# Ten kept-row slots, a new pace for the node tiles and evenly handed early products in the max-pooling layer of a graph network

## The chip, the cores and the metric

The kernel runs on one core of a Trainium2 chip. The metric is the device time of one execution in microseconds: the median of 3 runs, 2517.03 us (2515.44 to 2526.33). The core's engines run side by side, each through its own list of instructions in order: PE (matrix products; PEld is its weight load), DVE (vector), ACT (scalar), POOL (which issues the gathers) and SP (which issues plain transfers). They meet at semaphores.

## The reference

`x` has 6250 rows of 256, and 100000 edges lead from `src` to `dst` with `dst` sorted. The block is a layer norm with ReLU, then four graph layers and a last product:

```python
h = jnp.maximum(_layernorm(x, axis=-1), 0.0)
# layer 1, mean:   h @ W1_self + (segment_sum(h[src]) / deg) @ W1_neigh + b1
# layer 2, pool:   hp = relu(h @ W_pool + b_pool); hmax = segment_max(hp[src])
#                  h @ W2_self + hmax @ W2_neigh + b2
# layer 3, gcn:    ((segment_sum(h[src]) + h) / (deg + 1)) @ W3_neigh + b3
# layer 4, mean:   h @ W4_self + (segment_sum(h[src]) / deg) @ W4_neigh + b4
x = x + (h @ W_fc + b_fc)
```

All features inside are 512 wide. Layer 2 alone has a nonlinearity inside (the ReLU and the maximum). From its output on everything is linear, so the kernel multiplies the later weights into each other and carries layer 2's result times those products, in rows of 512 numbers.

## The kernel before

**Tiles and steps.** The 6250 nodes make NT = 49 tiles of 128; the edges make T = 782 groups of 128. Few low nodes take most edges (`dst` grows as a square), so sums into the first tiles ("hub" tiles) are done as products with a count matrix, whose blocks of 128 by 128 lie in `tab_a`; sums into the others gather rows.

**Prologue (to about 93 us).** Loads `x` in 17 groups of three tiles, normalizes them, turns the edge lists around (`pt_e`, `srcT`), finds where windows of edges begin (`pa`, with `SN` as input), and computes two weight products with `W2_pool` (`w2pf`): `pt_w` turns a weight block on PE, ACT copies it (`wT`), `pm_w` multiplies, ACT copies the result (`Wa`, `Wb`). A generator `products1` hands these steps out: line 1186 says how many after each group `g`. Layer 1 follows (to about 648 us).

**Layer 2, the pooling stage (about 648 to 1850 us).** One loop over 782 steps, counted by `at`, in six blocks from the last to the first (100, 130, 180, 220, 100 and 52 steps). Each step gathers 128 rows (POOL, L1803, into `X`, two steps to a buffer, six buffers) and takes running maxima on DVE (L1784); every second step SP stores a row of maxima (L1788). When a block ends, its *carry* goes from partition to partition: PE turns the last maxima (`ptcf`, L1524), DVE scans them, PE turns them back, and a row is stored. After that the node tiles whose edges begin in that block can be finished.

**Node tiles (`done2`, from tile 48 down to 1; tile 0 has its own function).** A tile gathers its maxima (`tot`, L1658), takes the maximum of two of them if its edges cross a block (DVE, L1678), turns them on PE (L1682), and multiplies with the merged weights in eight f32 products (L1689 and L1692 for its own part, L1695 for the maxima). ACT splits the result into a high part (`hi`, L1702) and a low part (`lo`, L1711). `row_parts(d)` says where these go: tiles 40 to 48 into a small pool, the others into slot `d % 11`, of which slots 0 to 7 lie in the tile `kept_rows` and three in a pool `early3`. Tiles 0 to 7 must end in `kept_rows`, since layer 3 reads them there. A tile is begun when it is ready, at least 11 steps have passed (7 in the last block) and fewer tiles are begun than `NT * (at - 112) / (T - 36 - 112)`, a straight line from step 112 to 746.

**Early products.** Layer 3 needs, for each of 23 hub tiles, a product over all node tiles. For node tiles 8 to 39 it is done early, inside the pooling stage: four finished tiles make a batch, and a batch gives 23 groups of four *pairs* (736 pairs in all). For each group SP loads blocks (`ae`, L1752, fourteen buffers), ACT widens them (`aw`, L1739), PE does pairs (L626 in f16 and L631 in f32), and DVE adds the sum to `acc` (L1435; the first batch is copied by ACT instead). For the hub tile's own row the pair is joined by two more products. From step 321 on, each step asks for a 48th of the pairs that are waiting (fewer steps near the end). A slot may be overwritten when all pairs of the tile that held it have been handed out; `over` has that number and an assertion checks it.

**What sets the order.** The code is written in the order above; a scheduler then orders the instructions of each engine by its own estimates. The order of SP, POOL, PE and ACT below is its result; DVE's in the prologue is fixed by hand.

## Time and profile before

| | |
|---|---|
| median of 3 runs | 2517.03 us (2515.44 to 2526.33) |
| profiled execution | 2523.93 us, span 2522.0 us, mean granted clock 0.933 |
| prologue and layer 1 | to about 648 us |
| pooling stage, first gather to last | 653 to 1803 us |
| layers 3 and 4 | about 1850 to 2522 us |
| busy share of the span | PE 86%, DVE 80%, POOL 69%, ACT 50% |

All positions are microseconds from the first instruction of the profiled execution. Busy time counts instructions that execute; an engine that waits for a semaphore is idle, and the bracket behind a row tells how long it had been idle and what ended that. A busy share near 1 tells that an engine has no gaps, not that nothing else could go faster.

### The profile page before, as it was taken

How to read it: one execution, taken by the hardware profiler on the slowest of the kernel's cores; microseconds unless marked ns; L12 is line 12 of the kernel's file. 1: busy time of each engine (PE TensorE's matmuls, PEld its weight loads, DVE VectorE, ACT ScalarE, POOL GpSimd, SP SyncE). 2: the span in 40 equal slices, each digit the busy share in tenths (PEclk: the TensorE clock that was granted, in tenths of full speed). 3: DMA queues.
4: the chain of work that ended last, by engine and by line, in shares of the span. 5: the costliest groups of instructions: out<-in, count | busy, mean ns of one | idle time of the engine just before them, and what ended most of it. 6: DMA issues, size and time to landing. Idle time of an engine off the chain costs nothing.

```text
span 2522.0 us, 35297 instructions
## 1 busy us (share of the span) xinstructions
PE 2158.2 (86%) x9402; PEld 1248.5 (50%) x9402; DVE 2010.3 (80%) x5565; ACT 1273.2 (50%) x2569; POOL 1729.6 (69%) x2013
## 2 busy tenths in 40 slices
PE   4699999999795565769999999896389999799997
PEld 2456666776443232334444444343244444477776
DVE  7899987785799898888889999798757777467665
ACT  4888888676488787765323333231112222244443
POOL 5477776667566777676667665677477777477775
PEclk9799999999897787789999999898799999899999
DMA  9677777777899999999999999999799999899997
GB/s 306 198 231 233 223 210 213 216 235 238 294 364 303 341 350 346 323 367 357 334 307 339 342 335 301 299 361 326 258 395 407 407 407 407 319 359 333 335 310 234
DMA packets 381357, 785.68 MB, mean 312 GB/s; under 512 B 56430, under 2 KB 175830, under 8 KB 381116
## 3 DMA queue, kind: packets, MB, share of 16 engines
q0 software_dynamic: 135184, 471.64, 56.0%
q1 hardware_dynamic: 158504, 221.70, 24.4%
q10 hardware_dynamic: 87460, 90.01, 10.7%
q8 instruction: 76, 1.25, 0.2%
q14 instruction: 133, 1.09, 0.1%
HBM read 573.99 MB, written 209.94 MB: 311 GB/s over the span
## 4 chain that ended last, share of the span: by engine, by line
PE 45%; DMA 27%; DVE 14%; issue 5%; ACT 5%; POOL 4%; ACTq 0%; DVEq 0%; POOLq 0%; SPq 0%
DMA X<-rows,srcIf 9%; PE pd L626 8%; PE pd L631 8%; PE pd L624 6%; DMA xq<-acc 5%; PE pm_prf L1695 3%; DVE run L1784 3%; DMA ring<-tab_s,srcE 3%; PE pm_hp L1271 3%; PE pm_prf L1689 2%; DMA rows<-X 2%; PE pm_hp L1265 2%; POOL X L1803 2%; PE pm_prf L1692 2%; PE pg L568 2%
## 5 line engine op out<-in xcount | busy, mean ns | idle before, releaser
L1803 POOL DMA_INDIRECT X<-rows,srcIf x782 | 742.7, 950 | 346.1 <-issue 148.8
L1784 DVE SCALAR_TENSOR_TENSOR run<-run,samef,X 128x512 f32<-128x512 f32 x758 | 572.9, 756 | 31.8 <-DMA X<-rows,srcIf 27.0
L548 POOL DMA_INDIRECT ring<-tab_h,srcT x402 | 389.6, 969 | 177.6 <-issue 39.9
L1912 ACT CAST af<-ac 128x640 fp32r<-128x640 fp8e4 (+2 forms) x299 | 217.2, 734 | 339.3 <-PE pd L624 121.7
L548 POOL DMA_INDIRECT ring<-tab_r,srcE x254 | 255.0, 1004 | 102.8 <-issue 35.1
L1784 DVE SCALAR_TENSOR_TENSOR X<-X,samef,run 128x512 f32<-128x512 f32 x379 | 281.9, 744 | 40.2 <-issue 19.7
L548 POOL DMA_INDIRECT ring<-tab_s,srcE x254 | 244.5, 963 | 93.0 <-issue 23.5
L602 DVE SCALAR_TENSOR_TENSOR acc<-pg,M,acc 128x256 f32<-128x256 f32 (+2 forms) x556 | 281.3, 533 | 31.6 <-PE pg L573 16.3
L573 PE MATMUL pg<-ring,hot 128*128 128x256 f32 (+1 forms) x656 | 292.2, 455 | 0.0
L631 PE MATMUL pd<-kept_rows,aw 128*128 128x512 f32 x529 | 271.0, 588 | 0.0
L1739 ACT CAST aw<-ae 128x512 fp32r<-128x512 fp8e4 x184 | 113.8, 620 | 252.1 <-PE pd L631 225.0
L570 PE MATMUL pg<-ring,hot 128*128 128x259 f16 (+1 forms) x656 | 211.5, 325 | 28.7 <-DMA ring<-tab_r,srcE 8.3
L626 PE MATMUL pd<-kept_rows,ae 128*128 128x512 f16 x529 | 208.5, 394 | 10.7 <-DMA ae<-tab_a 8.4
L1695 PE MATMUL pm_prf<-unf,hTf 128*128 128x512 f32 x384 | 196.9, 637 | 6.1 <-ACT hTf L1685 5.4
L631 PE MATMUL pd<-Z1h,af 128*128 128x256 f32 x588 | 194.8, 364 | 1.0 <-ACT af L1299 1.0
L544 DVE TENSOR_SCALAR hot<-iota_bf,keyE 128x128 fp32r<-128x128 bf16 x508 | 138.3, 300 | 48.2 <-PE pg L573 22.7
L624 PE MATMUL pd<-zt,af 128*128 128x512 f32 x598 | 166.3, 398 | 1.5 <-ACT af L1912 1.5
L626 PEld LDWEIGHTS <-ae 128*128 128x128 fp8e4 x736 | 71.3, 97 | 193.0 <-issue 176.6
L626 PE MATMUL pd<-Z1l,A 128*128 128x259 f16 x588 | 158.5, 280 | 0.0
L573 PEld LDWEIGHTS pg<-ring,hot 128*128 128x128 f32 x656 | 130.7, 199 | 47.7 <-issue 39.1
L624 PE MATMUL pd<-z,af 128*128 128x512 f32 x529 | 149.1, 400 | 2.8 <-ACT af L1912 1.5
L463 ACT ACTIVATE A<-pb 128x392 fp8e4<-128x392 f32 x240 | 116.2, 495 | 69.7 <-PE pb L457 65.7
(439 smaller groups left out, 5027.7 us busy)
## 6 DMA issues: line engine op xcount, KB each, us to landing
rows<-X SPq DMA_DIRECT2D x385, 256.0 KB
rows<-hpf SPq DMA_DIRECT2D x49, 256.0 KB
th<-tab_t ACTq DMA_DIRECT2D x49, 256.0 KB
X<-rows,srcIf POOLq DMA_INDIRECT x782
ae<-tab_a SPq DMA_DIRECT2D x184, 64.0 KB
tab_a<-A ACTq DMA_DIRECT2D x15, 784.0 KB
ac<-tab_a ACTq DMA_DIRECT2D x138, 80.0 KB
tab_t<-th SPq DMA_DIRECT2D x37, 256.0 KB
```

Source lines behind the costliest of these rows:

```text
L544: nc.vector.tensor_scalar(hot[j], iota_b, keyT[:, j - jb : j - jb + 1], None, op0=ALU.is_equal)
L548: nc.gpsimd.indirect_dma_start(out=ring[:, j % deep, :].bitcast(F32), out_offset=None, in_=table, in_offset=bass.IndirectOffsetOnAxis(ap=s ...
L570: nc.tensor.matmul(pg[:, : F + counts], hot[j].bitcast(BF16)[:, 1::2], X.bitcast(F16)[:, 2 * F : 3 * F + counts], start=(k == 0), stop=False)
L573: mm = nc.tensor.matmul(pg[:, :F], hot[j], X[:, :F], start=False, stop=(k == n - 1))
L602: nc.vector.scalar_tensor_tensor(acc[d], half, m, acc[d], op0=ALU.mult, op1=ALU.add)
L624: nc.tensor.matmul(hold[0], a[0], z, start=(s == ss[0]), stop=(s == ss[-1]))
L626: nc.tensor.matmul(hold[0][:, : F + extra], a[1], z[1][:, : F + extra], start=(s == ss[0]), stop=False)
L631: nc.tensor.matmul(hold[0][:, :F], a[0], z[0], start=False, stop=(s == ss[-1]))
L1695: nc.tensor.matmul(pm, hT[:, c, :], un[:, c, :], start=False, stop=(c == KH - 1))
L1784: nc.vector.scalar_tensor_tensor(put, held, st, row, op0=ALU.mult, op1=ALU.max)
L1803: nc.gpsimd.indirect_dma_start(out=X[:, k, :], out_offset=None, in_=tab_p, in_offset=bass.IndirectOffsetOnAxis(ap=srcI[:, t : t + 1], axis=0),
L1912: nc.scalar.copy(wide[i][:, :n, :], got[i][:, :n, :])
```

## The change

Five edits, all in the fast path:

1. `SLOTS = (10, 13)`: ten slots in `kept_rows` and 13 in all, where there were 8 and 11. A table `slot` is made for every tile: tiles 39 down to 4 take 0, 1, 2 ... 12, 0 and so on; tiles 3 to 0 take 0 to 3. `kept_rows` takes over the place of the merged weights' tile, which is as large, so no other tile is moved by it.
2. Instead of an assertion, `row_parts` hands out early products until the slot's former tile is done.
3. `PACE`: the limit on begun tiles is now a line with two kinks, 0 at step 112, 19 at step 318, 37 at 612, 49 at 746 (the straight line has 15.9 at 318 and 38.6 at 612). The least distance of 11 or 7 steps is kept.
4. From step 321 on, the early products handed out follow a straight line over all 736 pairs from step 320 to step 742, bounded by what is ready, in place of a 48th of what is waiting.
5. In the prologue the steps of `products1` begin at group 4, not 3, and two of them come with each of groups 7 to 13, not 7 to 12.

```diff
-FIRST_AT = 112
 EARLY_AT = 310
+SLOTS = (10, 13)
+PACE = ((112, 0), (318, 19), (612, 37), (746, 49))
...
-                for _ in range(2 if 7 <= g < 13 else g >= 3):
+                for _ in range(2 if 7 <= g < 14 else g >= 4):
                     next(steps, None)
...
         def row_parts(d):
-            i = d % ROWS3
-            assert early.done >= over.get(d + ROWS3, 0)
+            i = slot[d]
+            if d in held_by:
+                early.advance(over[held_by[d]])
...
-            if i < KEPT:
+            if i < SLOTS[0]:
                 return kept_rows[0][:, i, :], kept_rows[1][:, i, :]
...
-        ROWS3 = 2 * BATCH + 3
+        slot, held_by, last = {}, {}, {}
+        for d in reversed(range(NT)):
+            slot[d] = i = (EARLY[1] - 1 - d) % SLOTS[1] if d >= 4 else 3 - d
+            assert d >= KEPT or i < SLOTS[0]
+            if d < EARLY[1]:
+                if i in last:
+                    held_by[d] = last[i]
+                last[i] = d
+        assert all(d >= EARLY[0] for d in held_by.values())
+        early_all = H3 * (EARLY[1] - EARLY[0])
...
+        def paced(at):
+            for (a0, n0), (a1, n1) in zip(PACE, PACE[1:]):
+                if at < a1:
+                    break
+            return n0 + (n1 - n0) * (at - a0) / (a1 - a0)
...
-                        kept_rows += [span3.tile([P, KEPT, FH], dt, tag=f"kept{i}",
+                        kept_rows += [span3.tile([P, SLOTS[0], FH], dt, tag=f"kept{i}",
...
                     if at > EARLY_AT + 10:
-                        early.advance(early.done + math.ceil(
-                            early.left() / max(1, min(48, T - 24 - at))))
+                        early.advance(math.ceil(early_all * (at - EARLY_AT - 10)
+                                                / (T - 40 - EARLY_AT)))
...
-                            and begun2 < NT * (at - FIRST_AT) / (T - 36 - FIRST_AT)):
+                            and begun2 < paced(at)):
...
-            Z3 = {s: (kept_rows[0][:, s, :], kept_rows[1][:, s, :]) for s in range(KEPT)}
+            Z3 = {s: tuple(v[:, slot[s], :] for v in kept_rows) for s in range(KEPT)}
```

What this does to the engines' lists is shown at three places. (The changed file has one line more ahead of the first place and more further down, so its line numbers are higher: L1015 becomes L1016, L626 becomes L627, L1658 becomes L1660.) In layer 1 from its first gather on, and in layers 3 and 4, the lists are the same.

**PE in the prologue**, where the second turn of the edge lists (`pt_e`), the first weight product (`pm_w`) and the selections (`pa`) meet. Before:

```order
L1015 MATMUL pt_e<-identf,rF 128x128 x5
L285 MATMUL pt_w<-identf,wl 128x128 x4
L291 MATMUL pm_w<-w2pf,wT 128x512 x4
L1015 MATMUL pt_e<-identf,rF 128x128 x5
L932 MATMUL pa<-SN,sel_261 128x2
L934 LDWEIGHTS later
```

Changed:

```order
L1016 MATMUL pt_e<-identf,rF 128x128 x5
L933 MATMUL pa<-SN,sel_261 128x2
L935 LDWEIGHTS later
L935 MATMUL pa<-unit,later 128x2
L933 MATMUL pa<-SN,sel_261 128x2
L935 LDWEIGHTS later
L935 MATMUL pa<-unit,later 128x2
L933 MATMUL pa<-SN,sel_261 128x2
L1016 MATMUL pt_e<-identf,rF 128x128 x5
L286 MATMUL pt_w<-identf,wl 128x128 x4
L292 MATMUL pm_w<-w2pf,wT 128x512 x2
```

The second `pt_e` and the first selections now stand ahead of the first `pm_w`, of which two of four products follow here and two after more selections. On ACT the first copy `wT` moves behind the scaling of the sixth group.

**PE around the third block's carry** (`ptcf`, the block that ends with step 410). Before:

```order
L626 MATMUL pd<-kept_rows_11381,ae 128x512
L631 MATMUL pd<-kept_rows_11380,aw 128x512
L1695 MATMUL pm_prf<-unf,hTf 128x512 x2
L626 LDWEIGHTS ae
L626 MATMUL pd<-kept_rows_11381,ae 128x512
L631 MATMUL pd<-kept_rows_11380,aw 128x512
L626 LDWEIGHTS ae
L626 MATMUL pd<-r2l_15210,ae 128x512
L631 MATMUL pd<-r2h_15209,aw 128x512
L1524 MATMUL ptcf<-identf,X_15832 128x128 x4
```

Changed:

```order
L627 LDWEIGHTS ae
L627 MATMUL pd<-kept_rows_11381,ae 128x512
L632 MATMUL pd<-kept_rows_11380,aw 128x512
L627 LDWEIGHTS ae
L627 MATMUL pd<-kept_rows_11381,ae 128x512
L632 MATMUL pd<-kept_rows_11380,aw 128x512
L1525 MATMUL ptcf<-identf,X_15718 128x128 x4
```

Before, 195 pairs and 47 tile products (L1689, L1692, L1695) stand between the first pair and this carry, and a tile is under way when it comes; changed, 154 and 55, and the tile products lie further ahead. From here to the fourth block's carry it is 421 and 114 before, 446 and 112 changed; behind that, 120 and 54 before, 136 and 48 changed.

**POOL where the third block's node tiles gather their maxima** (`tot`; `rows_of_10235` belongs to the third block, `rows_of_10236` to the second, whose rows a tile takes too when its edges cross). Before:

```order
L1803 DMA X_16288<-rows_72,srcIf 128x512 x2
L1803 DMA X_16308<-rows_72,srcIf 128x512 x2
L1658 DMA tot<-rows_72,rows_of_10235 128x512
L1658 DMA tot<-rows_72,rows_of_10236 128x512
L1658 DMA tot<-rows_72,rows_of_10235 128x512
L1658 DMA tot<-rows_72,rows_of_10236 128x512
L1803 DMA X_16333<-rows_72,srcIf 128x512 x2
```

Changed:

```order
L1820 DMA X_16036<-rows_72,srcIf 128x512 x2
L1820 DMA X_16063<-rows_72,srcIf 128x512 x2
L1660 DMA tot<-rows_72,rows_of_10235 128x512
L1660 DMA tot<-rows_72,rows_of_10236 128x512
L1660 DMA tot<-rows_72,rows_of_10235 128x512
L1820 DMA X_16087<-rows_72,srcIf 128x512 x2
L1660 DMA tot<-rows_72,rows_of_10236 128x512
```

The gathers stand behind 452 steps' gathers before and behind 440 in the change, and a pair of steps stands between the third and the fourth. The corresponding gathers of the fourth block stand behind 652 in both.

## The prediction

> **What bounds the kernel now.** I read the page first, then the busy time by stretches, then the waits by engine, then single rows. The page:
>
> ```profile
> span 2522.0 us, 35297 instructions
> PE 2158.2 (86%) x9402; PEld 1248.5 (50%) x9402; DVE 2010.3 (80%) x5565; ACT 1273.2 (50%) x2569; POOL 1729.6 (69%) x2013
> L1803 POOL DMA_INDIRECT X<-rows,srcIf x782 | 742.7, 950 | 346.1 <-issue 148.8 <-DVE run L1784 59.6 <-DVE X L1784 33.2
> ```
>
> Layer 2's pooling, with its 782 gathers (L1803), is nearly half of the span and is where all three numbers of the change's title act. The rest of the program, layer 1 from its first gather on and layers 3 and 4, keeps its instructions in the same rows on every engine; only the prologue and the pooling stage differ. So I cut the pooling stage where the change works: from the first early product (1132) to the third block's carry on PE (1275), from there to the fourth block's carry (1590), then the stall behind it, then the rest. Columns are busy time and instructions of PE, PEld, DVE, ACT, POOL, then granted clock, DMA share, GB/s; the second table is POOL's gathers of L1803 alone.
>
> ```profile
> 1132.00:1275.00 143.00, 139.19 (x511) 66.16 (x512) 122.67 (x220) 56.69 (x105) 97.46 (x104) 0.97 0.99 343
> 1275.00:1590.00 315.00, 310.66 (x1178) 151.42 (x1176) 287.35 (x428) 98.58 (x179) 209.89 (x222) 0.99 0.96 323
> 1590.00:1640.00 50.00, 37.43 (x116) 17.58 (x116) 36.86 (x64) 9.39 (x19) 34.17 (x37) 0.86 0.92 307
> 1640.00:1745.00 105.00, 83.47 (x298) 40.68 (x297) 95.32 (x140) 23.26 (x44) 75.74 (x81) 0.90 0.98 338
> ...
> 1132.00:1275.00 143.00, 94.35 (x100) 0.97 0.99 343
> 1275.00:1590.00 315.00, 195.69 (x207) 0.99 0.96 323
> 1590.00:1640.00 50.00, 24.72 (x27) 0.86 0.92 307
> 1640.00:1745.00 105.00, 71.97 (x77) 0.90 0.98 338
> ```
>
> A gather takes 143/100 = 1.43 us in the first stretch, 315/207 = 1.52 in the second and 105/77 = 1.36 in the last. The slow stretches are those in which PE has no gap. Whether PE is really full there is settled by spacing, not by busy time:
>
> ```profile
> 1274.83 0.60 PE L1524 MATMUL ptcf<-identf,X 128*128 128x128 f32 x4
> 1322.32 0.39 PE L626 MATMUL pd<-kept_rows,ae 128*128 128x512 f16 x1
> 1322.78 0.39 PE L626 MATMUL pd<-kept_rows,ae 128*128 128x512 f16 x1
> 1589.38 0.60 PE L1524 MATMUL ptcf<-identf,X 128*128 128x128 f32 x4
> ...
> 1205.46 1.72 PE pm_prf L1689 x4
> ...
> 1249.35 0.75 DVE L1784 SCALAR_TENSOR_TENSOR X<-X,samef 128x512 f32<-128x512 f32 x1
> 1588.44 0.75 DVE L1784 SCALAR_TENSOR_TENSOR X<-X,samef 128x512 f32<-128x512 f32 x1
> ```
>
> An early product is a pair (L626 and L631), and pairs start 0.46 us apart. A tile product (L1689, L1692, L1695) is f32 and runs as two rows of 1.72/4 = 0.43, so 0.86; eight make a node tile. What the second stretch holds:
>
> ```profile
> L631 PE MATMUL pd<-kept_rows,aw 128*128 128x512 f32 x312 | 156.6, 577 | 0.0
> L1435 DVE TENSOR_TENSOR acc<-acc,pd 128x512 f32<-128x512 f32 x106 | 72.6, 685 | 16.4 <-PE pd L631 15.1
> L631 PE MATMUL pd<-r2h,aw 128*128 128x512 f32 x110 | 59.9, 581 | 0.0
> L1695 PE MATMUL pm_prf<-unf,hTf 128*128 128x512 f32 x112 | 52.6, 592 | 0.0
> L1689 PE MATMUL pm_prf<-usA,th 128*128 128x512 f32 x60 | 29.4, 608 | 0.0
> L1692 PE MATMUL pm_prf<-usB,th 128*128 128x512 f32 x56 | 27.1, 607 | 0.0
> ```
>
> That is 422 pairs and 228/2 = 114 tile products: 422 x 0.465 + 114 x 0.86 = 294 us, with some 17 for transposes and own rows 311, of the 314.6 between the two carries. PE is the bound there; DVE, 91% busy, waits 15.1 us for it, and POOL's gathers wait for DVE. DVE ends a block with the rows at 1249.35 and 1588.44: at the third carry PE is 25 us behind it, at the fourth the two are level, so DVE is a close second.
>
> **The change, part by part.** *Slots, pace and even handing (one answer).* The work is the same, its place moves. Counted in PE's order between the same carries: from the first pair to the third carry 195 pairs and 47 tile products now, 154 and 55 changed; from the third to the fourth carry 421 and 114 now, 446 and 112 changed, and four own-row pairs fewer (11 to 7); behind the fourth carry 120 and 54 now, 136 and 48 changed, with the four own rows.
>
> - First stretch: -41 x 0.465 + 8 x 0.86 = -12.2 us.
> - Second: 25 x 0.465 - 2 x 0.86 - 4 x 0.465 = +8.0 us.
> - Behind the fourth carry: 16 x 0.465 - 6 x 0.86 + 4 x 0.465 = +4.1 us.
>
> The first two are one full run of PE, so the fourth carry comes 4.2 us earlier. The 4.1 us behind it are hidden: PE idles 12.6 + 21.5 = 34 us between 1590 and 1745; without that cover they would give the gain back. So -4.2 for the stage. Bounds: DVE's wait for PE in the whole stage, all removed, is -20; the second stretch's +8.0 with the first's saving lost, and the +4.1 exposed, is +12. Near the sum lies a third price: were DVE the bound, its four additions fewer ahead of the fourth carry's tiles (134 now, 130 changed) would give 4 x 0.685 = -2.7. I take the sum, since PE has only 3.8 us without work in the first stretch.
>
> Two stalls stay, where DVE's maximum stands behind tile gathers that POOL issues late:
>
> ```profile
> 1309.89 0.69 DVE L1678 TENSOR_TENSOR tot<-tot 128x512 f32<-128x512 f32 x1 [5.63 <-DMA tot<-rows,rows_of]
> 1618.02 0.69 DVE L1678 TENSOR_TENSOR tot<-tot 128x512 f32<-128x512 f32 x1 [9.26 <-DMA tot<-rows,rows_of]
> ...
> SPq L1752 <- PE pd L626: 165.5, 134, 2.7
> POOL X L1803 <- DMA rows<-X: 23.7, 56, 2.5
> DVE acc L1435 <- PE pd L631: 20.2, 54, 1.0
> ```
>
> The first moves with its gathers, 12 steps earlier, the second keeps its place: 0. On SP, the early loads (L1752) wait for PE with the stores of X behind them; POOL's share of that is 23.7 us. The loads keep their distance to the stores within a step or two: 0 again. The two more kept slots cost nothing: every copy and store into them was there before.
>
> *The prologue's products, one group later.*
>
> ```profile
> 33.47 6.46 PE L291 MATMUL pm_w<-w2pf,wT 128*128 128x512 f32 x8 [11.01 <-DMA w2pf<-in_L_gnn_W_pool]
> 43.78 3.68 PE L291 MATMUL pm_w<-w2pf,wT 128*128 128x512 f32 x8
> 34.75 0.43 DVE L808 BATCH_NORM_STATS2 st<-xt 128x6 f32<-128x256 f32 x1 [5.05 <-DMA xt<-in_x]
> 35.09 0.15 DVE L830 SCALAR_TENSOR_TENSOR nb<-mv,rs 128x3 f32<-128x3 f32 x1
> 40.40 0.89 DVE L1019 CAST srcT<-pt_e 128x512 int32<-128x512 f32 x2 [3.16 <-PE pt_e L1015]
> 39.96 0.60 ACT L298 ACTIVATE Wa<-pm_w 128x512 f32<-128x512 f32 x1 [11.47 <-PE pm_w L291]
> 47.99 1.57 ACT L832 ACTIVATE xt<-xt,nb,rs 128x256 f32<-128x256 f32 x3
> 20.00:30.00 10.00, 2.15 (x9) 1.78 (x9) 9.59 (x34) 5.70 (x12) 5.23 (x6) 1.00 1.03 367
> 30.00:40.00 10.00, 6.53 (x11) 2.91 (x12) 2.46 (x9) 0.04 (x1) 0.00 (x0) 1.00 1.11 340
> ```
>
> Now PE stands 11 us in front of pm_w, which waits for w2pf, and the second pt_e stands behind it; DVE waits 3.16 us for that pt_e. In the changed order pt_e comes first, so that wait goes. The 5.05 us for xt just before it stay (that is a transfer). What is late next is ACT: its copy wT, moved behind the sixth group's scaling, can end at about 35.1 + 1.6 + 0.2 + 0.6 = 37.6; at 6.46 us pm_w then ends near 44.1, and with the selections between its halves 44.7. Wa and wT (0.6 each) come after it, so the scaling of the eighth group starts at 45.9, where 47.99 - 3.16 = 44.8 was open: 1.1 us of the 3.16 go back, -2 remain. Bounds: at 3.68 us for pm_w -3.2; if the transfers set the pace (DMA share 1.03 and 1.11 here), 0. I take -2.
>
> [...]
>
> Sum: -4.2 - 2 = -6.2 us. The profiled execution took 2523.93 us (span 2522.0), 6.9 more than the median 2517.03, so it becomes about 2517.7, and the median 2511.
>
> **The rivals.**
> - *B, the heavier second stretch decides (slower).* If gathers and not PE set the first stretch's pace (it runs at 1.43 us per gather, near the last stretch's 1.36), PE's 12.2 us there become idle time, the third carry stays at 1275, and the second stretch gets 8.0 us longer: +8, with the 4.1 us behind exposed +12; median 2525 to 2529. It decides once PE idles over 8 us between the first pair and the third carry. Against it: PE idles 3.8 us there now, and 12 us are less than the 25 us by which it lags at the third carry.
> - *C, the waits go with the peak (much faster).* If steady handing takes away DVE's 20.2 us of waiting for PE, the stage gets 20 us shorter and the median is 2495. For it: 1.36 us a gather is reached when PE is not full. Against it: the changed order has more pairs, not fewer, in the longest full stretch.
> - *D, PE is not the bound and the prologue is the transfers'.* Then the moved pairs change nothing in either stretch and the wait of 3.16 turns into one for xt: 0, 2517.
>  [...] The spacing of pairs in the trace speaks against it: 311 of 314.6 us are accounted for.
> - *That it doesn't do what it says:* in the order, the handing is hardly more even. Of DVE's 161 additions 134 stand ahead of the fourth carry's tiles now and 130 in the change, which is why I expect little.
>
> **How the numbers follow.** Forecast 0.46, B 0.20, C 0.20, D 0.14. A measurement of this kernel cannot tell less than 0.5% (12.6 us) from no change. Faster than that: C and a tail of the forecast, 0.26. Slower: half of B and 0.02 for something unseen, 0.12. Within: 0.62. The range reaches from C's 2495 to B's upper 2529, a little in from both as their prices are upper bounds for one mechanism: 2494 to 2528. The forecast's own range, from the prologue's 0 to -3.2 and the stage's 0 to -8, is 2506 to 2517.
>
> **What would show it.** Prologue: pt_e and srcT without the 3.16 us wait and the first gather of layer 1 about 2 us earlier (D: a wait for xt there). Stage: third carry on PE about 12 us earlier than 1275 less the prologue's gain, and the stretch to the fourth carry about 8 us longer; B shows PE idle over 8 us ahead of the third carry; C shows under 1.45 us per gather in the second stretch and less than 5 us of DVE waiting for PE. Behind the fourth carry 27 + 77 gathers in about the same 155 us, or the 4.1 us are not hidden. Wrong altogether would be a change in layers 3 and 4, or a wait of ACT's casts for a row slot that is still held.

## The result

The changed kernel takes 2512.73 us (median of 10 runs, 2505.66 to 2517.65), the kernel before 2523.42 us beside it (10 runs, 2515.44 to 2528.7). The ratio is 0.9957, with a 95% interval of 0.994 to 0.9974: faster by 0.26% to 0.6%, or 7 to 15 us. So these twenty runs tell less than the 0.5% that the prediction took for the least. The forecast was 2511 us, by a gain of 6.2 on the 2517.03 us of three earlier runs. The measured time is 1.7 us from it. But ten runs put the kernel before at 2523.42, and the gain is 10.7 us. Most of the working behind the forecast did not come out, as the stretches show, so the close number is luck.

### The profile page after: what moved, and what is told of

It reads as the page before. It is cut to its first block, busy times and chain, and to the rows that moved or that the text cites. A ratio compares the mean times of both kernels' runs of the same rounds, so it can differ in the third digit from the quotient of the medians.

```text
span 2510.6 us, 35310 instructions
## 1 busy us (share of the span) xinstructions
PE 2150.9 (86%) x9402; PEld 1248.1 (50%) x9402; DVE 2008.0 (80%) x5565; ACT 1272.9 (51%) x2569; POOL 1728.4 (69%) x2013
## 3 DMA queue, kind: packets, MB, share of 16 engines
q10 hardware_dynamic: 87460, 90.01, 10.7%
## 4 chain that ended last, share of the span: by engine, by line
PE 47%; DMA 28%; DVE 14%; issue 4%; ACT 3%; POOL 3%; ACTq 0%; SPq 0%; POOLq 0%; DVEq 0%
DMA X<-rows,srcIf 10%; PE pd L627 8%; PE pd L632 8%; PE pd L625 7%; DMA xq<-acc 6%; PE pm_prf L1697 3%; PE pm_hp L1272 3%; DVE run L1795 2%; PE pm_w L292 2%; DMA ring<-tab_s,srcE 2%; PE pm_hp L1266 2%; PE pm_prf L1691 2%; PE pm_prf L1694 2%; PE pg L569 2%; DMA rows<-X 2%
## 5 line engine op out<-in xcount | busy, mean ns | idle before, releaser
L1820 POOL DMA_INDIRECT X<-rows,srcIf x782 | 743.0, 950 | 338.2 <-issue 143.1
L549 POOL DMA_INDIRECT ring<-tab_s,srcE x254 | 243.8, 960 | 92.7 <-issue 22.5
L1795 DVE SCALAR_TENSOR_TENSOR X<-X,samef,run 128x512 f32<-128x512 f32 x379 | 281.7, 743 | 31.5 <-issue 10.8
L632 PE MATMUL pd<-kept_rows,aw 128*128 128x512 f32 x598 | 304.8, 588 | 0.0
L627 PE MATMUL pd<-kept_rows,ae 128*128 128x512 f16 x598 | 235.5, 394 | 23.7 <-DVE acc L1436 14.3
L1697 PE MATMUL pm_prf<-unf,hTf 128*128 128x512 f32 x384 | 191.8, 622 | 9.7 <-ACT hTf L1687 9.3
L627 PEld LDWEIGHTS <-ae 128*128 128x128 fp8e4 x736 | 71.7, 97 | 191.4 <-issue 177.1
L627 PE MATMUL pd<-Z1l,A 128*128 128x259 f16 x588 | 158.5, 280 | 0.1
L346 ACT ACTIVATE many<-A,less 128x1536 fp8e4<-128x1536 fp8e4 (+1 forms) x92 | 147.3, 1601 | 4.2 <-issue 2.2
```

The costliest lines, as they stand in the source:

```text
L346: nc.scalar.activation(many[:, : s1 - s0, :], A[:, s0:s1, :], AF.Relu, bias=less, accum_out=most[:, at : at + 1], saturate=False)
L549: nc.gpsimd.indirect_dma_start(out=ring[:, j % deep, :].bitcast(F32), out_offset=None, in_=table, in_offset=bass.IndirectOffsetOnAxis(ap=s ...
L627: nc.tensor.matmul(hold[0][:, : F + extra], a[1], z[1][:, : F + extra], start=(s == ss[0]), stop=False)
L632: nc.tensor.matmul(hold[0][:, :F], a[0], z[0], start=False, stop=(s == ss[-1]))
L1697: nc.tensor.matmul(pm, hT[:, c, :], un[:, c, :], start=False, stop=(c == KH - 1))
L1795: nc.vector.scalar_tensor_tensor(put, held, st, row, op0=ALU.mult, op1=ALU.max)
```

## The profile after

The profiled execution took about 2512.5 us. Its page, for comparison with the three lines shown of before:

```profile
span 2510.6 us, 35310 instructions
PE 2150.9 (86%) x9402; PEld 1248.1 (50%) x9402; DVE 2008.0 (80%) x5565; ACT 1272.9 (51%) x2569; POOL 1728.4 (69%) x2013
L1820 POOL DMA_INDIRECT X<-rows,srcIf x782 | 743.0, 950 | 338.2 <-issue 143.1
```

Nothing got cheaper: the engines are as busy as before to within 0.4%. The gathers' idle time fell from 346.1 to 338.2 us. Where the stage is cut as in the prediction, first by the rows that cut it (PE's first early pair, the third, fourth and fifth carry, then DVE's last row of the third and fourth block):

```profile
1116.55 0.61 PE L627 MATMUL pd<-kept_rows,ae 128*128 128x512 f16 x1 [6.82 <-DMA ae<-tab_a]
1256.39 1.06 PE L1525 MATMUL ptcf<-identf,X 128*128 128x128 f32 x4
1577.34 0.61 PE L1525 MATMUL ptcf<-identf,X 128*128 128x128 f32 x4
1727.95 1.08 PE L1525 MATMUL ptcf<-identf,X 128*128 128x128 f32 x4 [15.87 <-DVE X L1795]
...
1233.44 0.75 DVE L1795 SCALAR_TENSOR_TENSOR X<-X,samef 128x512 f32<-128x512 f32 x1
1576.43 0.74 DVE L1795 SCALAR_TENSOR_TENSOR X<-X,samef 128x512 f32<-128x512 f32 x1
```

Before, these rows stood at 1132.24, 1274.83, 1589.38, 1737.01, 1249.35 and 1588.44. Two of them the prediction does not show; with them, layer 2's first gather, before and changed:

```profile
1132.24 0.61 PE L626 MATMUL pd<-kept_rows,ae 128*128 128x512 f16 x1 [8.39 <-DMA ae<-tab_a]
1737.01 1.09 PE L1524 MATMUL ptcf<-identf,X 128*128 128x128 f32 x4 [20.38 <-DVE X L1784]
...
653.03 0.98 POOL L1803 DMA_INDIRECT X<-rows,srcIf  x1 [17.91 <-DMA col<-in_L_gnn_b]
...
649.67 0.99 POOL L1820 DMA_INDIRECT X<-rows,srcIf  x1 [15.61 <-DMA col<-in_L_gnn_b]
```

So:

| stretch | before, us | changed, us | difference | forecast |
|---|---|---|---|---|
| start to layer 2's first gather | 653.03 | 649.67 | -3.4 | -2 |
| to the first early pair | 479.2 | 466.9 | -12.3 | 0 |
| to the third carry | 142.6 | 139.8 | -2.8 | -12.2 |
| to the fourth carry | 314.6 | 320.9 | +6.4 | +8.0 |
| to the fifth carry | 147.6 | 150.6 | +3.0 | 0 (4.1, hidden) |
| to the end of the span | 785.0 | 782.7 | -2.3 | 0 |

In the stretches that the change is about, the changed kernel loses 6.6 us where 4.2 were to be won. It wins 12.3 us in a stretch for which the prediction had no term. The view that cuts the stage into these stretches shows what the first of them holds (columns as in the prediction: busy time and instructions of PE, PEld, DVE, ACT, POOL, then granted clock, DMA share, GB/s). Behind it stand POOL's gathers of L1820 alone in the first stretch, PE's waits in that stretch (changed, then before), and DVE's waits for gathered rows from the first pair to the fifth carry (changed, then before):

```profile
1116.00:1256.00 140.00, 127.38 (x448) 61.87 (x449) 113.54 (x204) 53.10 (x102) 96.04 (x103) 0.95 0.99 345
1256.00:1577.00 321.00, 318.44 (x1207) 154.52 (x1205) 291.58 (x440) 99.52 (x178) 210.19 (x223) 0.99 0.95 318
...
1116.00:1256.00 140.00, 92.25 (x99) 0.95 0.99 345
...
PE pd L627 <- DVE acc L1436: 9.5, 2, 5.5
...
PE pd L626 <- DVE acc L1435: 3.6, 2, 2.7
...
DVE run L1795 <- DMA X<-rows,srcIf: 20.2, 11, 5.4
...
DVE run L1784 <- DMA X<-rows,srcIf: 10.6, 11, 1.3
```

PE's busy time in the first stretch fell from 139.19 to 127.38 us: 11.8 of the 12.2 us that were counted. But the stretch kept nearly its length, and PE spent most of the time waiting for DVE to add a sum. The gathers kept their pace, 140/99 = 1.41 us each, where it had been 143/100 = 1.43. One of PE's two waits (5.5 us) ended when DVE came through its maxima, which it ran without a gap; the other (3.9 us) stood behind a maximum that had itself waited 5.4 us for its gathered rows. In the second stretch PE is as full as before (318.44 of 321), and the stretch grew by nearly what the count says.

DVE's own waits for PE rose:

```profile
DVE acc L1436 <- PE pd L632: 31.7, 70, 2.0
```

They were 20.2 us in 54 waits. Evenly handed products did not take these waits away; there are more of them.

## The experiments

Two theories and their rivals were set against each other. *P*, the prediction's: PE's rows set the stretches, and moved rows move the time. *G* and *V*: the gathers, or DVE, set the pace where PE is not full. *W*: the gain is the new pace's, ahead of the first pair, by node tiles begun sooner. *N*: that part differs from one execution to the next by chance.

The experiments ran in four groups on three chips (chip 7: e1 to e4, and later x4 and r4; chip 8: r1, r2; chip 4: x1, x2, x3, r3). In all four the kernel before took 2964 to 2971 us, not 2523; the chip of the first comparison is not recorded. The last section shows what differs. The ratio in the table is the recorded one, not the quotient of the two medians. A ratio there has an interval of about plus or minus 0.27%, 8 us, so by time alone the runs tell large effects only. Each has a profile, and the places of its rows tell more.

| run | median, us | before, us | ratio, 95% interval |
|---|---|---|---|
| e1, prologue alone | 2975.02 | 2971.39 | 0.9995 (0.997 to 1.002) |
| e2, prologue undone | 2974.06 | 2971.39 | 0.9998 (0.9966 to 1.0029) |
| e3, old handing | 2978.01 | 2971.39 | 1.0002 (0.9978 to 1.0027) |
| e4, straight pace | 2968.75 | 2971.39 | 1.0000 (0.9974 to 1.0025) |
| r1, changed | 2962.37 | 2971.23 | 0.9970 (0.9944 to 0.9997) |
| r2, straight pace again | 2972.17 | 2971.23 | 0.9999 (0.9974 to 1.0024) |
| x1, one product | 2943.59 | 2963.94 | 0.9908 (0.9879 to 0.9937) |
| x2, narrow sums | 2969.27 | 2963.94 | 1.0014 (0.9988 to 1.0041) |
| x3, bent handing | 2964.97 | 2963.94 | 0.9994 (0.9968 to 1.0020) |
| r3, changed again | 2961.44 | 2963.94 | 0.9999 (0.9970 to 1.0028) |
| x4, both less | 2940.47 | 2970.86 | 0.9905 (0.9874 to 0.9935) |
| r4, the kernel before | 2972.23 | 2970.86 | 0.9994 (0.9965 to 1.0023) |

**The prologue (e1, e2).** Edit 5 alone in the kernel before, and everything but edit 5:

```diff
-                for _ in range(2 if 7 <= g < 13 else g >= 3):
+                for _ in range(2 if 7 <= g < 14 else g >= 4):
```

> The kernel before with edit 5 alone: the steps of products1 begin at group 4 and two of them come with groups 7 to 13. Layer 2 is the kernel before's, row by row. Theory P (the prediction): DVE's 3.16 us wait for the second pt_e goes and ACT gives 1.1 back, so the first gather of layer 1 comes about 2 us earlier and the time is 2 us below the kernel before (ratio 0.9992). Theory D (the transfers of x set the prologue's pace): the wait turns into a longer wait for xt; 0 us, ratio 1.000. In the changed kernel's trace the wait for xt grew from 5.05 to 6.03 us and its first int cast stood 1.24 us earlier before any edited row, so between the two I expect -0.5 us.

> The changed kernel with edit 5 undone (products1 as in the kernel before); the pooling stage is the changed kernel's, row by row. Theory P: 2 us above the changed kernel, so 8 to 9 us below the kernel before (ratio 0.9965). Theory D: level with the changed kernel (ratio 0.9957), so that the whole gain is the pooling stage's.

The times tell neither apart (0.9995 and 0.9998). The place of layer 1's first gather does: here in the changed kernel's first trace, in e1, in e2, and in r4, which is the kernel before:

```profile
91.75 1.01 POOL L549 DMA_INDIRECT ring<-tab_h,srcT  x1 [24.78 <-DVE dB L1036]
...
90.48 1.16 POOL L548 DMA_INDIRECT ring<-tab_h,srcT  x1 [25.42 <-DMA tab_t<-tho]
...
95.92 0.94 POOL L549 DMA_INDIRECT ring<-tab_h,srcT  x1 [25.33 <-PE pb L404]
...
95.65 0.99 POOL L548 DMA_INDIRECT ring<-tab_h,srcT  x1 [25.88 <-PE pb L403]
```

Eleven traces have the new prologue, and their first gather stands between 90.48 and 92.53. Three have the old one: 93.37, 95.65 and 95.92. All eleven are earlier than all three, by 3.4 us in the mean (1.6 in the first pair of traces). This part of the change is shown for the place of that gather: about the forecast's 2 us, with 3.4 just beyond the bound of 3.2. That the time follows is not shown.

**Handing and pace, one at a time (e3, e4, r2).** In e3 the handing alone is the old one, in e4 the pace alone:

```diff
-                        early.advance(math.ceil(early_all * (at - EARLY_AT - 10)
-                                                / (T - 40 - EARLY_AT)))
+                        early.advance(early.done + math.ceil(
+                            early.left() / max(1, min(48, T - 24 - at))))
```

```diff
-PACE = ((112, 0), (318, 19), (612, 37), (746, 49))
+PACE = ((112, 0), (746, 49))
```

> The changed kernel with edit 4 undone: from step 321 each step asks for a 48th of the waiting pairs again; slots and pace stay. In PE's order 209 pairs and 55 tile products stand between the first pair and the third carry (154 and 55 in the changed kernel), 402 and 108 with 10 own rows to the fourth (446, 112, 7), 125 and 52 behind it (136, 48). Theory P (PE's rows set both stretches): first stretch 55 x 0.465 = 25.6 us longer than in the changed kernel, second 44 x 0.465 + 4 x 0.86 - 3 x 0.465 = 22.5 us shorter, time 3 us above the changed kernel. Theory G (where PE is not full the gathers set the pace at about 1.4 us each): the first stretch grows only from 139.8 us to PE's own 157, +17, the second shrinks only to about 309, -12, and some 3 us come back behind the fourth carry: +2, the same time but other stretches. Theory W (the gain is the pace's, ahead of the first pair) wants the part ahead of the first pair to stay as early as in the changed kernel, 12.6 us before the kernel before after layer 1 is taken out.

> The changed kernel with edit 3 undone: the limit on begun tiles is the straight line from step 112 to 746 again; slots, even handing and prologue stay. Between the first pair and the third carry 154 pairs and 47 tile products (55 in the changed kernel), to the fourth 446 and 119 (112), behind it 136 and 49 (48). Theory P (PE's rows set both stretches): first stretch 8 x 0.86 = 6.9 us shorter, second 7 x 0.86 = 6 us longer, so the changed kernel's time within 1 us. Theory W (what the changed kernel gained, it gained ahead of the first pair, by tiles begun sooner, 18.9 and not 15.9 by step 318): the 9 us between layer 1 and the first pair are lost, the first stretch stays at about 139 us since PE is not full there, the second gets 6 us longer: 9 to 15 us above the changed kernel, level with the kernel before or above it. Theory N (that part of the trace differs by chance from one execution to the next): the part ahead of the first pair stays within 3 us of the changed kernel's.

> The changed kernel itself once more, as the control that the first four runs lacked: on their chip the kernel before took 2971 us, not 2517, with idle time in places where the profiles shown had none. Where the chip is like the first one, theory P and theory W both say 0.9957 of the kernel before, the first gather of layer 1 some 1.6 us and the first early pair some 15 us earlier than in the kernel before. Theory N (the places differ by chance from one execution to the next) would show it by another distance ahead of the first pair: then the 15.7 us are no property of the change. Where the chip is like the second, the ratio tells how much of the 0.4% is left there: by theory P, which needs a full PE, nothing.

> The changed kernel with the straight line for the begun tiles (edit 3 undone), once more beside the changed kernel on one chip. Theory P: within 1 us of the changed kernel. Theory W: the 9 us between layer 1 and the first pair are lost, the first stretch stays near 139 us, the second gets 6 us longer: 9 to 15 us above the changed kernel. Theory N: within 3 us of the changed kernel, and the first pair within 3 us too.

The first pair, the third and the fourth carry in r3 (the changed kernel), in e3 and in r4 (the kernel before):

```profile
1344.11 0.38 PE L627 MATMUL pd<-kept_rows,ae 128*128 128x512 f16 x1
1506.68 1.05 PE L1525 MATMUL ptcf<-identf,X 128*128 128x128 f32 x4
1874.56 0.61 PE L1525 MATMUL ptcf<-identf,X 128*128 128x128 f32 x4
...
1364.99 0.39 PE L627 MATMUL pd<-kept_rows,ae 128*128 128x512 f16 x1 [2.35 <-issue]
1562.64 0.60 PE L1525 MATMUL ptcf<-identf,X 128*128 128x128 f32 x4
1917.31 0.60 PE L1525 MATMUL ptcf<-identf,X 128*128 128x128 f32 x4
...
1352.71 0.39 PE L626 MATMUL pd<-kept_rows,ae 128*128 128x512 f16 x1
1535.09 0.60 PE L1524 MATMUL ptcf<-identf,X 128*128 128x128 f32 x4
1908.96 0.60 PE L1524 MATMUL ptcf<-identf,X 128*128 128x128 f32 x4
```

Read in the same way in every trace of these chips, the stretches to the third, fourth and fifth carry are (means where several traces have the same lists there):

| lists of the stage | to the third | to the fourth | to the fifth | sum | P says of the first two, against the changed kernel |
|---|---|---|---|---|---|
| changed (r1, r3, e2) | 165.3 | 371.0 | 184.7 | 721.0 | |
| before (r4, e1) | 177.3 | 374.2 | 179.1 | 730.7 | +12.2, -8.0 |
| old handing (e3) | 197.7 | 354.7 | 179.2 | 731.6 | +25.6, -22.5 |
| straight pace (e4, r2) | 154.5 | 387.9 | 184.8 | 727.2 | -6.9, +6.0 |
| bent handing (x3) | 175.5 | 360.4 | 179.8 | 715.7 | +12.1, -14.0 |

Against the changed kernel, the rows measured are +12.0 and +3.2, +32.4 and -16.3, -10.8 and +16.9, +10.2 and -10.6. In the first stretch, the count of PE's rows tells the sign four times out of four and the size to within 7 us; executions of one list differ there by 5 to 10 us. In the second it has the sign three times and misses the kernel before's, and r4 alone misses what was expected of it in both stretches (182.4 and 373.9 us). Theory G, by which e3's first stretch grows by 17 us and x3's not at all, is off in both, in x3 by about what two executions can differ by. So where PE *stands* at a carry is indeed set by what its list holds. But a longer stretch there is in the main one with more gathers in it: counted in the traces, e3's first stretch holds 110, the changed kernel's 97 or 98, e4's 88, all at 1.66 to 1.81 us each. PE's carry moves against the gathers more than the gathers move. That the *time* follows is not shown: e3 and e4, whose third carries stand 44 us apart, differ by 9 us in time, and each is level with the kernel before within its interval.

Theory W falls on these chips, as far as the runs can tell. Layer 2's first gather and the first pair in two executions of the very same program, r1 and then r3:

```profile
785.15 0.96 POOL L1820 DMA_INDIRECT X<-rows,srcIf  x1 [23.64 <-DMA weights<-in_L_gnn_W_fc]
1363.68 0.61 PE L627 MATMUL pd<-kept_rows,ae 128*128 128x512 f16 x1 [3.26 <-DMA ae<-tab_a]
...
790.07 0.96 POOL L1820 DMA_INDIRECT X<-rows,srcIf  x1 [23.61 <-DMA col<-in_L_gnn_b]
1344.11 0.38 PE L627 MATMUL pd<-kept_rows,ae 128*128 128x512 f16 x1
```

That is 578.5 and 554.0 us for one list of instructions. To step 330 the eight traces with the new pace take 569 us in the mean and the four with the old one 567, with standard deviations of 9 and 6 us. So two executions can well differ by the 12.3 us of the first comparison; the pace alone (all but it in e4 and r2: 1.0000 and 0.9999) is not shown to bring them. In the first two traces 3.6 of the 12.3 us are there by the 191st gather (269.4 us behind the first before, 265.8 changed), and from layer 2's first gather up to there the lists of PE, ACT and POOL are the same. One more piece can be named. In the kernel before, soon after gather 260, DVE waits for PE in front of a counting mask (`hm`), because PE stands at a tile product (L1689) that waits for the load of `th`:

```profile
1029.74 3.78 PE L1689 MATMUL pm_prf<-usA,th 128*128 128x512 f32 x4 [3.56 <-DMA th<-tab_t]
1033.72 0.27 DVE L441 TENSOR_SCALAR hm<-iota_w,mkR 128x196 bf16<-128x196 f16 x1 [3.72 <-PE pb L457]
```

In the changed kernel the tiles there begin four steps sooner, PE waits 1.75 us for `th` and DVE has no wait of over 1 us for PE. That is 3.7 us of the 12.3, in one execution.

**What PE's and DVE's rows are worth (x1, x2, x4).** If PE is the bound, work taken from it must show. In x1 the f16 product of an early pair is left out, in x2 DVE adds 64 of 512 columns, in x4 both:

```diff
-                nc.tensor.matmul(hold[0][:, : F + extra], a[1], z[1][:, : F + extra],
-                                 start=(s == ss[0]), stop=False)
+                both = not light or s == own
+                if both:
+                    nc.tensor.matmul(hold[0][:, : F + extra], a[1], z[1][:, : F + extra],
+                                     start=(s == ss[0]), stop=False)
```

```diff
-            nc.vector.tensor_add(acc3[d], acc3[d], v)
+            nc.vector.tensor_add(acc3[d][:, :64], acc3[d][:, :64], v[:, :64])
```

> The changed kernel, where an early pair is its f32 product alone: the f16 product is left out (but for the hub tile's own row), so the sums lack the low parts. PE has 736 x 0.23 = 171 us less to do in the pooling stage; gathers, DVE and ACT's work stay. Theory P (PE's rows set the two stretches up to the fourth carry): the stage becomes DVE's and the gathers'. At the last stretch's 1.36 us a gather the 307 gathers of the two stretches take 418 us where the changed kernel takes 461: about 40 us less (1.5%). [...] Theory G (PE sets the second stretch alone, the first is the gathers'): 207 x 1.36 = 282 for 321, some 35 us less, all in the second stretch.

> The changed kernel, where DVE adds 64 of the 512 columns of each early sum (161 additions): the other columns of the sums are left out. DVE has some 161 x 0.5 = 80 us less to do in the pooling stage, PE and the gathers have the same. Theory P (PE sets the two stretches up to the fourth carry): the stage gets shorter behind the fourth carry alone, by at most 40 additions x 0.5 = 20 us. A theory V (DVE, 91% busy in the second stretch, is the bound there and PE only follows it): 40 us or more less, half of the 80. The scheduler answers with another order (375 pairs and not 446 up to the fourth carry), so by P there is 33 us less for PE in the second stretch, which it does later.

> The changed kernel itself once more, beside the three others on one chip, so that they can be set against it. By its first comparison 0.9957 of the kernel before; on a chip as slow as the last two 0.996 to 0.999. For the places: stretch from the first pair to the third carry 140 us and to the fourth 321 us on a chip like the first one, about 166 and 373 on one like the last two.

> Both cuts at once: an early pair is its f32 product alone (PE 171 us less) and DVE adds 64 of 512 columns of each early sum (DVE some 80 us less); the low parts and the other columns are left out of the sums. One cut alone gave 27 us below the kernel before in its run (PE) and nothing (DVE). If PE and DVE take turns as the bound, both together give much more than 27 us: 60 to 80 below the kernel before (ratio 0.973 to 0.98). If the gathers themselves and what the engines idle without a waiter (51 idle times of over 1.5 us on PE in the changed kernel's run on these chips, one on the first) set the stage's pace, it stays near the PE cut's 27 us (ratio 0.988 to 0.992).

Busy times of x1, x2 and, for comparison, r3 on the same chip; then x1's second stretch, in the columns of the stretches above:

```profile
PE 2120.8 (72%) x8681; PEld 1260.3 (43%) x8681; DVE 2010.2 (68%) x5565; ACT 1273.2 (43%) x2569; POOL 1729.1 (59%) x2013
...
PE 2276.0 (77%) x9402; PEld 1301.8 (44%) x9402; DVE 1944.1 (66%) x5565; ACT 1274.6 (43%) x2569; POOL 1737.5 (59%) x2013
...
PE 2272.5 (77%) x9402; PEld 1294.4 (44%) x9402; DVE 2016.8 (69%) x5565; ACT 1275.2 (43%) x2569; POOL 1728.2 (59%) x2013
...
1522.00:1892.00 370.00, 223.29 (x737) 132.28 (x736) 297.08 (x451) 93.21 (x171) 220.96 (x234) 0.82 0.89 287
```

x1 takes 152 us of busy time from PE and is 18 us faster than the changed kernel beside it (2943.59 against 2961.44), or 27 us (0.92%) faster than the kernel before. That is less than theory P's 40, and not nothing. x2 takes 73 us from DVE and is no faster (1.0014). Both together give 0.9905, what PE's cut gives alone.

The runs differ from the changed kernel by more than the cut: the scheduler answered with other orders. x1 has 223, 421 and 92 pairs where the changed kernel has 154, 446 and 136, and x2 has 375 between the third and the fourth carry, as was expected of it. With that limit, neither PE nor DVE is the bound of the stage in these runs, and they do not take turns either. In x1 the second stretch has 147 us in which PE does nothing, and it is still 370 us long; it holds 218 gathers where r3's 368 us hold 208, so 1.70 us a gather in place of 1.77. What is the bound was not tried: the share of the DMA engines stays at 0.89 in x1's second stretch, and no run takes gathers or other transfers away. By this measure a microsecond of PE's rows is worth 18/152 to 27/152, some 0.12 to 0.18 us, and the 12.2 us moved out of the first stretch 1.5 to 2.2. As a statement on the time, theory P has fallen in these runs, and V with it, within that limit.

In the prediction PE counted as full in the second stretch by the spacing of its pairs (311 of 314.6 us accounted for). In r3's second stretch PE is busy 329.19 of 368 us, 89%, and x1, with 152 us less in the whole run, is 18 us faster: PE had room there, though not so much that taking work from it gave nothing.

**A better line (x3) and the kernel before against itself (r4).**

```diff
+HAND = ((320, 0), (410, 180), (630, 490), (742, 736))
-                        early.advance(math.ceil(early_all * (at - EARLY_AT - 10)
-                                                / (T - 40 - EARLY_AT)))
+                        early.advance(math.ceil(paced(at, HAND)))
```

> The changed kernel, with a bent line for the early products in place of the straight one: 0 at step 320, 180 pairs asked for by step 410, 490 by 630, 736 by 742. In PE's order 180 pairs stand between the first pair and the third carry (154 in the changed kernel), 416 to the fourth (446), 140 behind it (136); the tile products stay. Theory G (the first stretch is the gathers' in the changed kernel, with 11 us of PE idle in it, the second is PE's): the first stretch stays at 140 us, the second gets 30 x 0.465 = 14 us shorter, or 7 where DVE takes over: 7 to 14 us below the changed kernel. Theory P (PE's rows set both): +12.1 and -14.0, 2 us below the changed kernel.

> The kernel before against itself: 1.000, and how far 12 runs on these chips stray from it (the intervals so far say 0.27%, 8 us). Its profile stands beside those of the changed kernel on such chips. By theory P its stretch from the first pair to the third carry is longer than the changed kernel's (162 to 167 us, first pair counted from its f16 product or f32 product alike), about 172 to 177, the next one shorter, 360 to 365 where the changed kernel has 368 to 376. The first gather of layer 1 by the prediction 2 us later than in the changed kernel (91.0 to 92.3 in three executions with the new prologue): 93 to 94.

x3 fills the first stretch and relieves the second. Its three stretches together are 715.7 us, 5 below the changed kernel's mean; but that is one trace, and the changed kernel's three range from 712.5 (r3) to 732.3 (r1). The time is 0.9994 of the kernel before, beside 0.9999 for the changed kernel: they are not told apart, and no version is shown to beat the change. r4 came out at 0.9994, inside its interval, so 0.06% is what two sets of runs of one program differ by here.

Over r1 and r3 the changed kernel has 24 timed executions with a mean of 2963.4 us (standard error 2.3); the kernel before has 113 in the four groups with 2969.9 (1.0). The difference of 6.5 us (0.22%) has a standard error of 2.5 and goes the way of the first comparison. But r1 and r3 ran on chips 8 and 4; against the 55 executions of the kernel before on these two alone it is 4.7 us, with a standard error of 2.6, which is not clear of noise. On chip 8 the ratio was 0.9970, on chip 4 0.9999.

## Why the prediction was right in its number and not in its working

- **Prologue, -2: right in size, by the later traces.** In the first two traces layer 1's first gather is 1.6 us earlier, and the other 1.8 of the table's -3.4 came in layer 1, whose lists did not change. Of the 1.6, 1.24 were there before any edited row (DVE's first cast of `rF`, at 18.50 and 19.74). It is the eleven traces against three that show the term; in r3 and r4 that cast stands at 18.67 and 18.78, and the first gather at 91.05 and 95.65. DVE's row of `srcT`, which had waited 3.16 us, now follows without a wait. The wait for `xt` ahead of it grew a little, from 5.05 to 6.03 us, which is rival D's sign and a third of its size:

```profile
34.36 0.43 DVE L809 BATCH_NORM_STATS2 st<-xt 128x6 f32<-128x256 f32 x1 [6.03 <-DMA xt<-in_x]
36.77 0.88 DVE L1020 CAST srcT<-pt_e 128x512 int32<-128x512 f32 x2
...
37.08 3.78 PE L292 MATMUL pm_w<-w2pf,wT 128*128 128x512 f32 x4 [5.32 <-ACT wT L289]
42.19 3.64 PE L292 MATMUL pm_w<-w2pf,wT 128*128 128x512 f32 x4
```

  The two halves of `pm_w` take 3.78 + 3.64 = 7.4 us where the whole took 6.46. So splitting did not make it shorter, and the second half ends at 45.8 where the prediction has 44.7. A row of the first half takes 0.95 us and one of the second 0.91, where the later eight rows of before take 3.68/8 = 0.46. The -2 reckons with the 6.46 us and not with the 3.68; why it should be the one or the other was the author's estimate, and no run shows it. Idle time of PE ahead of the rows does not sort the traces: the first half comes after 5.32 us of idle and the second without a wait; in r4 the first eight rows take 5.21 us after 13.45 us of idle, and the next eight, at 44.03, take 5.38 without a wait. The granted clock reads 1.00 from 30 to 40 us in both of the first traces.
- **First stretch, -12.2: the step that failed.** PE's rows got 11.8 us shorter, nearly as counted, and the stretch 2.8. The sentence "I take the sum, since PE has only 3.8 us without work in the first stretch" is the error: PE was 97% busy there, and yet the gathers kept their pace when it had less to do (1.43 us each, then 1.41). PE's waits for DVE's additions went from 3.6 to 9.5 us and its idle time from 3.8 to 12.6, beyond the 8 us at which rival B was to decide. B's mechanism fits what happened there, with 9.4 of its 12.2 us, and the three stretches together, +6.6, are near its +8. What holds the gathers is not shown. It is not DVE's work alone, as DVE was 86% busy there before (122.67 of 143) and 81% after (113.54 of 140), with longer waits for gathered rows; the DMA share is 0.99 in both. And this is one pair of traces: in the experiments' runs the changed kernel's first stretch is 12.0 us shorter in the mean, as the prediction has it, and its second is 3.2 us shorter, not 8 longer.
- **Second stretch, +8.0: +6.4 measured.** The term was right in these two traces.
- **Behind the fourth carry, "hidden under 34 us of idle PE": +3.0 of the 4.1 came out.** The cover was idle time of PE. That the rows there are waited for by others before that idle time comes is an argument from the order; no run tests it.
- **DVE's stalls in front of the tile maxima, 0.** From the first pair to the fifth carry they were 17.8 us in 4 waits before and are 11.5 in 3 in the changed kernel. These 6 us went to the good, and the stretches that hold them still got longer.
- **The early loads' place among the stores, 0.** POOL's waits for stores of `X` were 23.7 us and are 31.2 over the whole program, and the early loads' waits for PE went from 165.5 to 191.5 us. Whether that costs time is not shown.
- **Rival C** is excluded: 321/208 = 1.54 us a gather in the second stretch, not under 1.45, and 31.7 us of waiting for PE, not under 5. **Rival D** was right in one half, on the chips of the experiments: PE is not what the stage's time hangs on (x1: 18 to 27 us for 152), though in the prologue a wait did go.
- **What had no step.** The 12.3 us ahead of the first pair carry the result. The lists there differ by one tile begun four steps sooner, and the prediction counted only what stands behind step 320. 3.7 us of it are explained, and 3.6 came where the lists are the same. The rest is within what one execution of one program strays from the next in the later runs, while the gain of 7 to 15 us over twenty runs is too sure to be chance. What it is made of stays open: no run of an experiment was like those of the first comparison, where the kernel before takes 2523 us.

So the sum of -6.2 had, by the first two traces, two right terms (-2, +8.0), one that was over four times too large (-12.2) and one too small (0 behind the fourth carry), and lacked what outweighed these. By its own terms as measured, -3.4 - 2.8 + 6.4 + 3.0, the result would have been +3.2, a forecast of no gain.

## What to carry to other kernels

A count of an engine's rows between two marks tells where that engine will stand at the marks, here to within 7 us in the first stretch and up to 11 us off in the second; what it does to the time is told only by an experiment that takes rows away from it, and here 152 us of PE's work were worth 18 to 27. Before a term is taken at full price, ask what else keeps the stretch at its length: PE was 97% busy in the first one, and with 11.8 us less to do it made the stretch 2.8 us shorter, at nearly the same pace of the gathers. And put the unchanged kernel in every group of runs and compare two executions of one program, stretch by stretch, before a difference of 10 us between two traces is given a cause.

## What the runs showed that was not expected

The kernel before takes 2964 to 2971 us in the experiments' runs, on three chips, and 2523 in the first comparison, with the same busy times: DVE 2016.9 us in r4 and 2010.3 in the first trace, ACT 1275.2 and 1273.2, POOL 1733.2 and 1729.6. PE's is 5% up (2275.6 against 2158.2), at a mean granted clock of 0.888 against 0.933. The time is in the gaps. In the first traces nearly every long idle time of PE has a releaser. In r1, the changed kernel, it often has none:

```profile
586.87 0.49 PE L458 MATMUL pb<-hm,hs 128*128 128x196 bf16 x2 [6.42 <-issue]
...
PE pb L458 <- issue: 60.8, 33, 6.4
```

Counted over the whole span, PE stands over 1.5 us without anything to wait for 50 times in r1, 162 us together, and once, 5.2 us, in the first trace of the same program. ACT and DVE then wait for PE or for releasers that the profile doesn't know: in r3, from 1340 to 2140 us, ACT's copies `aw` 166.5 us for PE and 72.4 for such releasers, DVE's additions 62.1 and 51.7. Layer 1, which the change doesn't touch, takes 693 to 704 us from its first gather to layer 2's, not 558. The prologue takes as long as in the first traces, to layer 1's first gather 91.05 us in r3 and 91.75 in the first trace of that kernel. What holds the engines back between instructions was not tried and is left open. It may also be why the stage hangs so little on PE or DVE there, so how far x1's price holds where the kernel takes 2523 us is not known.
